# Splitting layer 1's front: batch norm and group norm two images ahead, layer norm and projection one image ahead

## The chip, the cores and the metric

The kernel runs on one core of one Trainium2 chip. The time is device microseconds (us) of one execution, the median of three runs. One more execution was profiled, with every instruction's start and end on each engine. The engines are TensorE (PE, matrix multiplies and transposes; PEld are its weight loads), VectorE (DVE), ScalarE (ACT), GpSimd (POOL) and SyncE (SP, which here issues every transfer between memory and the core's buffers).

## The reference

Four layers act on 16 images of 192 channels by 32 x 32 pixels (1024 tokens), all in float32, each as `x = x + layer(group_norm(x))`. Layer 0 is an mLSTM block with a 3 x 3 convolution and a batch norm over all images, layer 2 a depthwise convolution with batch norm, layer 3 a selective scan over four directions. Layer 1, which the change concerns, is a Mamba block on tokens:

```python
x = x + layer1(group_norm(x))            # 32 groups of 6 channels
# layer1(xf):
xn = layernorm(xf)                       # over the 192 channels
xm, z = split(xn @ in_proj_w.T)          # 384 + 384 channels
xc = silu(causal_conv1d(xm, 4 taps))
dt, B, C = split(xc @ x_proj_w.T);  dt = softplus(dt @ dt_proj_w.T + b)
h = exp(dt * A) * h + (dt * xc) * B      # a scan over 1024 tokens, 16 states
y = (sum_n h * C + xc * D) * silu(z)
out = layernorm(y @ out_proj_w.T + skip_scale * xf) @ proj_w.T + proj_b
```

## The kernel before

Each layer keeps channels on partitions (96 or 128 of them) and tokens along the free dimension. Layers 1 and 2 run together in `layer12`, one image after another. The core of it is `scan_run` (L942): one **step** is one of the 16 states of one half image (512 tokens), so an image is two units of 16 steps, 32 steps in all, and the stage has 512. A step does, for three tiles t of 128 channels, on ACT the decays (`da`, L987) and the products `xbt` (L967), on PE the transposes and a diagonal matmul into `xb` (L995, L998), on DVE the scan itself (`h`, L1011), on POOL the product with C (L1018), and two steps later on PE the sum over states into `y` (L1029). The tiles `xb` (3 PSUM buffers), `da` (5), `h` and `cb` (4) and `xbt` (2) say how far an engine can run ahead of the others.

All other work of layers 1 and 2 lies in generators that `Side.tick` (L221) advances while the steps are emitted. `side.add(kind, generator, start, end)` spreads a generator between two step numbers, in the units that its `yield`s give; `at` is 32 times the image. For an image b of the scan these are: `prep` (the projections to dt, B, C of the next unit), `gate` and `out` (the output projection of b - 1), `silu` (`layer1_gate`, the projection to z of b, L1287), `front` of b + 1, `tail` of b - 1 (layer norm, projection and residual, L1325), `conv` of b + 1 (L1263), and `layer 2` of b - 1 (L1360). That is the order of the program's text. The framework then orders each engine's queue by its own estimates of when an instruction can run; only the scan's matmuls on PE are tied to the text's order (`in_order`). On each engine the instructions then run in that order, and each waits at the head of its queue for what it needs. Side matmuls share two PSUM buffers named `mm`; the small tile `o` has two buffers, which `front` (L1257), `gate` (L1140), `tail` (L1336) and `layer 2` (L1370) take in turn.

`layer1_front` (L1223) is one generator in the kernel before. For one image it loads x into a tile called `x1` and layer 0's output into `xf` (L1227, L1229); applies layer 0's batch norm and leaky ReLU to `xf` and adds it to x (L1234 on ACT, L1235 and L1236 on DVE); stores the sum for the residual (L1238); takes group statistics (`group_norm`: L351 and L352 on DVE, L355 on PE, L357 to L362 on DVE, L365 on PE, L367 and L368 on ACT); writes the normalised image into `xf` (L1241) and stores it (L1242). From there it goes straight on to the layer norm, whose result `xn` is put into the tile `x1` again, and to the projection into the `xin` rows in memory (L1254, L1258, L1259). `xn` is read once more a good half image later, by the projection to z (L1298), and `x1` has one buffer: the next image's x can't be loaded before that projection's last matmul. The tile `xt`, also of one buffer, belongs to `out` and `tail`: it is loaded with the stored normalised image (L1311) and is free when the tail has written its own normalised image (L1352).

Of the kernel before, what the change touches and what calls it, by code (L numbers as in the profile page):

```python
# [10 lines left out]
F32 = mybir.dt.float32  # L11
# [8 lines left out]
HP = 96  # L20
DI = 384
S = 1024
# [167 lines left out]
def halves(n=S, step=512):  # L190
    return [slice(i, i + step) for i in range(0, n, step)]


def finish(steps):

    while True:
        try:
            next(steps)
        except StopIteration as end:
            return end.value  # L200
# [74 lines left out]
class Program:  # L275
# [795 lines left out]
    def layer12(self):  # L1071
        tc = self.tc
        with (
            tc.tile_pool(name="w1", bufs=1) as wp,
            tc.tile_pool(name="s1", bufs=2) as sp,
            tc.tile_pool(name="b1", bufs=2) as bp,
            tc.tile_pool(name="d1", bufs=3, space=DRAM) as dp,
            tc.tile_pool(name="ps1", bufs=2, space=PSUM) as psum,
        ):
            self.layer1_weights(wp, dp, psum)  # L1080
            self.rep = 18 * (W + 2), 6
            self.stats = wp.tile([HP, 2, 2 * self.nb, 6], F32, name="stats")
            self.image = {b: {} for b in range(self.nb)}
            side, units = Side(), []
            w_x = [self.w_x[:, t] for t in range(3)]

            def prep(u):
                xt = bp.tile([128, 4, DI], F32, name="xtok", bufs=1)
                xc = self.image[u.b]["xc"]
                rows = yield from self.scan_rows(xc[:, :, 512 * u.half : 512 * u.half + 512], w_x, 1, bp, dp, psum)  # L1090
                yield from self.scan_prep(u, rows, 0, xc, xt, True, self.w_dt, bp, psum)

            carry = [wp.tile([128, NS, 3], F32, name=f"carry{i}") for i in range(2)]
            for b in range(self.nb):
                for half in range(2):
                    c = carry[b % 2]
                    u = Unit(b, half, False, False, c if half else None, None if half else c)
                    u.neg_a = lambda t, n: self.neg_a[:, t * NS + n : t * NS + n + 1]
                    u.finish = lambda y, u=u: self.layer1_sum(u, y, bp)
                    units.append(u)  # L1100
            for b in range(self.nb):
                at = 2 * NS * b
                side.add("prep", prep(units[2 * b + 1]), at + 1, at + 13)
                if b:
                    side.add("gate", self.layer1_gated(units[2 * b - 1], bp, psum), at + 2, at + 3.5)
                    side.add("out", self.layer1_out(b - 1, bp, psum), at + 3.5, at + 8)
                side.add("silu", self.layer1_gate(b, bp, psum), at + 8, at + 12.5)
                if b + 1 < self.nb:
                    side.add("front", self.layer1_front(b + 1, sp, bp, psum), at + 12.5, at + 20)
                if b:  # L1110
                    side.add("tail", self.layer1_tail(b - 1, sp, bp, dp, psum), at + 13.5, at + 25)
                side.add("gate", self.layer1_gated(units[2 * b], bp, psum), at + 18, at + 21)
                if b + 1 < self.nb:
                    side.add("conv", self.layer1_conv(b + 1, bp, psum), at + 20, at + 26)
                if b:
                    side.add("layer 2", self.layer2(b - 1, bp, psum), at + 25.5, at + 34)
                if b + 1 < self.nb:
                    side.add("prep", prep(units[2 * b + 2]), at + 26, at + 30)
            finish(self.layer1_front(0, sp, bp, psum))
            finish(self.layer1_conv(0, bp, psum))  # L1120
            finish(prep(units[0]))
            self.scan_run(units, side, bp, psum)
            finish(self.layer1_gated(units[-1], bp, psum))
            finish(self.layer1_out(self.nb - 1, bp, psum))
            finish(self.layer1_tail(self.nb - 1, sp, bp, dp, psum))
            finish(self.layer2(self.nb - 1, bp, psum))
            self.batch_norm(sp, "2gamma", "2beta", self.bn2)
# [95 lines left out]
    def layer1_front(self, b, sp, bp, psum):  # L1223

        nc = self.nc
        x = bp.tile([HP, 2, S], F32, name="x1", bufs=1)
        nc.sync.dma_start(x, self.ins["x"][b].rearrange("(m p) t -> p m t", p=HP))  # L1227
        xf = bp.tile([HP, 2, S], F32, name="xf", bufs=1)
        nc.sync.dma_start(xf, self.y0[b].rearrange("(m p) t -> p m t", p=HP))  # L1229
        yield Wait(1)  # L1230
        for m in range(2):
            for h in halves():
                v = xf[:, m, h]
                nc.scalar.activation(v, v, AF.Identity, bias=self.bn0[:, m, 1:2], scale=self.bn0[:, m, 0:1])  # L1234
                nc.vector.scalar_tensor_tensor(v, v, 0.01, v, MUL, MAX)  # L1235
                nc.vector.tensor_tensor(x[:, m, h], x[:, m, h], v, ADD)  # L1236
                yield 0.5
        nc.sync.dma_start(self.x1[b], x)  # L1238
        mean, r, _ = yield from self.group_norm(sp, psum, x)
        for m in range(2):  # L1240
            nc.vector.tensor_scalar(xf[:, m], x[:, m], mean[:, m : m + 1], r[:, m : m + 1], SUB, MUL)  # L1241
        nc.sync.dma_start(self.xf1[b], xf)  # L1242
        yield 1
        xn = x
        for h in halves():
            yield from self.layer_norm(
                bp, psum, [xf[:, m, h] for m in range(2)], [xn[:, m, h] for m in range(2)],
                self.k("ones192", HP), HP, 512,
            )
        for t in range(3):  # L1250
            for h in halves():
                ps = psum.tile([128, 512], F32, name="mm")
                for m in range(2):
                    nc.tensor.matmul(  # L1254
                        ps, self.w_in[:, m, t * 128 : (t + 1) * 128], xn[:, m, h], start=m == 0, stop=m == 1
                    )
                o = bp.tile([128, 512], F32, name="o")  # L1257
                nc.scalar.activation(o, ps, AF.Identity, bias=self.b_in[:, t : t + 1])  # L1258
                nc.sync.dma_start(self.xin[b % 2][t][:, 3 + h.start : 3 + h.stop], o)  # L1259
                yield 1.7  # L1260
        self.image[b]["xn"] = xn
# [450 lines left out]
```

## Time and profile before

| | us |
|---|---|
| time, median of 3 runs (lowest to highest) | 17126.98 (17106.91 to 17131.63) |
| time of the profiled execution | 17158.12 |
| its span, first to last instruction | 17156.3 |
| layer 1 and 2's stage: first scan to layer 3's first scan | 3755 to 7541 |
| of this, an image in the middle (b = 8): 5534.6 to 5762.4 | 227.8 |
| layer 3: 7541 to 17156 | 9615 |

The page gives each engine's busy time and its share of the span, then the span in 40 slices, the chain that ended last, and the costliest groups of instructions. A group's line has the source line, the engine, the operation, what it writes and reads, how often it ran, then busy time, mean duration in ns, idle time of the engine before it, and what ended that. Step boundaries are the starts of the first scan (L1011 on DVE) of each step. Of the middle image b = 8: step 13 starts at 5614.3, step 17 at 5645.1, step 21 at 5690.6, step 27 at 5724.9, and the next image at 5762.4.

### The profile page before, as it was taken

The page shows a single profiled execution, that of the slowest core. Times are in us where ns is not written, and L with a number is a line of the kernel's source. Part 1 is how long each engine was busy: PE and PEld are TensorE (multiplying, and loading weights), DVE is VectorE, ACT ScalarE, POOL GpSimd, SP SyncE. Part 2 cuts the span into 40 slices and gives each one's busy share as a digit, 9 for nine tenths or more (in the row PEclk, how much of TensorE's full clock was granted, in tenths as well). Part 3 has the DMA queues.
Part 4 walks back from the last instruction along what each step waited for, and adds up shares of the span by engine and source line. Part 5 has one row for each costly group of instructions (what it writes and reads, how often), then busy time and mean ns, then how long its engine had stood idle before and what let it go on. Part 6 is the DMA issues. An engine that isn't in the chain of part 4 may idle for free. (4 is left out here: it accounts for less than half of the span.)

```text
span 17156.3 us, 262939 instructions
## 1 busy us (share of the span) xinstructions
PE 15613.4 (91%) x99452; PEld 10979.0 (64%) x99452; DVE 13102.8 (76%) x14795; ACT 11895.7 (69%) x19766; POOL 11422.4 (67%) x5491
## 2 busy tenths in 40 slices
PE   7999999979999999979999999999999999999998
PEld 4444444446555555647777777777777777777777
DVE  4555455547777777758888888988888898888888
ACT  3333333337666766748888888888888888888888
POOL 3334443436555555638888888878888888888888
PEclk8999999989999999989999999999999999999999
DMA  1111111123334443333333323333332333333232
GB/s 52 45 47 45 47 45 46 42 76 108 117 119 121 120 120 115 100 101 107 93 96 101 109 83 101 109 91 97 100 108 84 101 109 92 96 100 107 86 98 67
DMA packets 890140, 1544.64 MB, mean 90 GB/s; under 512 B 83472, under 2 KB 314653, under 8 KB 879530
## 3 DMA queue, kind: packets, MB, share of 16 engines
q1 hardware_dynamic: 888874, 1527.81, 29.7%
q8 instruction: 788, 12.91, 0.3%
q14 instruction: 478, 3.92, 0.1%
HBM read 1284.22 MB, written 243.27 MB: 89 GB/s over the span
## 5 line engine op out<-in xcount | busy, mean ns | idle before, releaser
L1018 POOL TENSOR_TENSOR h<-h,cb 128x1536 f32<-128x1536 f32 x2560 | 8871.5, 3469 | 1439.4 <-DVE h L1011 961.0
L987 ACT ACTIVATE da<-dt,neg_a 128x512 f32<-128x512 f32 x7680 | 5267.1, 714 | 1618.4 <-DVE h L1011 1565.5
L1011 DVE TENSOR_TENSOR_SCAN h<-da,carry,xb 128x512 f32<-128x512 f32 x3840 | 4653.2, 1263 | 708.8 <-PE xb L998 672.9
L1029 PE MATMUL y<-const,h 128*128 128x128 f32 x30720 | 4710.0, 276 | 127.4 <-DVE ysum L1469 54.0
L1011 DVE TENSOR_TENSOR_SCAN h<-da,xb 128x512 f32<-128x512 f32 x3840 | 4440.8, 1202 | 388.3 <-PE xb L998 272.1
L995 PE MATMUL xb<-const,xbt 128*128 128x128 f32 x23040 | 4057.7, 281 | 379.4 <-DVE h L1011 219.9
L967 ACT ACTIVATE xbt<-ut,bt 128x384 f32<-128x384 f32 x7680 | 4174.4, 603 | 210.3 <-PE xb L995 208.7
L1029 PEld LDWEIGHTS y<-const,h 128*128 128x128 f32 x30720 | 3677.9, 143 | 343.6 <-issue 288.4
L995 PEld LDWEIGHTS xb<-const,xbt 128*128 128x128 f32 x23040 | 2750.2, 142 | 1744.0 <-issue 616.2
L998 PE MATMUL xb<-diag,ut 128*128 128x128 f32 x15360 | 3015.1, 278 | 0.0
L998 PEld LDWEIGHTS xb<-diag,ut 128*128 128x128 f32 x15360 | 2382.8, 195 | 97.9 <-issue 97.9
L831 POOL TENSOR_TENSOR hs<-h,mhm 128x384 f32<-128x384 f32 x128 | 108.5, 848 | 1570.7 <-DVE den L836 735.6
L977 POOL TENSOR_TENSOR diag<-const,bt 128x512 f32<-128x512 f32 x640 | 687.0, 1074 | 575.3 <-PE xb L998 320.8
L1017 POOL COPY carry<-h 128x3 f32<-128x3 f32 x1280 | 249.1, 195 | 1222.7 <-DVE h L1011 978.2
L705 POOL TENSOR_TENSOR e<-e,const 128x1536 f32<-128x1536 f32 x128 | 443.3, 3464 | 244.0 <-DMA e<-row 226.9
L520 PE MATMUL conv<-ya,w_conv 128*64 128x512 f32 (+1 forms) x1152 | 500.9, 646 | 99.4 <-DMA ya<-yrows 61.2
L917 PE MATMUL mm<-dbl,w_dt 45*128 45x512 f32 x960 | 536.1, 642 | 33.4 <-DVE v L1491 16.1
L711 ACT ACTIVATE e<-e 128x1536 f32<-128x1536 f32 x128 | 189.7, 1482 | 445.6 <-POOL e L706 445.6
L780 PEld LDWEIGHTS num<-v,p 128*128 128x128 f32 x3072 | 386.6, 200 | 123.6 <-issue 50.8
L921 DVE SCALAR_TENSOR_TENSOR dt<-lnsq,mm 128x512 f32<-128x512 f32 x480 | 322.2, 671 | 184.1 <-ACT lnsq L920 184.1
L1172 PE MATMUL mm<-rep,taps 128*32 128x512 f32 x3072 | 423.8, 607 | 27.9 <-DMA rep<-xr 17.8
L1172 PE MATMUL mm<-rep,t_dw 96*32 96x512 f32 x2304 | 427.0, 618 | 22.1 <-DMA rep<-xr 15.9
(273 smaller groups left out, 17446.6 us busy)
## 6 DMA issues: line engine op xcount, KB each, us to landing
cb<-row SPq DMA_DIRECT2D x2560, 256.0 KB
rep<-xr SPq DMA_DIRECT2D x384, 331.0 KB
e<-row SPq DMA_DIRECT2D x128, 768.0 KB
rep<-xin SPq DMA_DIRECT2D x384, 256.0 KB
rep<-xr SPq DMA_DIRECT2D x384, 228.8 KB
x<-x SPq DMA_DIRECT2D x48, 768.0 KB
xr<-xin SPq DMA_DIRECT2D x48, 612.5 KB
xr<-xpad SPq DMA_DIRECT2D x32, 867.0 KB
```

Source lines behind the costliest of these rows:

```text
L520: nc.tensor.matmul(o, self.w_c2[:k, t, c0 : c0 + o.shape[0]], src[:k, r0 : r0 + 16, dx : dx + W], start=t == 0, stop=t == 14, skip_group_c ...
L705: nc.gpsimd.tensor_tensor(k.e, k.e, self.k0("mask")[:, None, :].to_broadcast([128, NH, 128]), ADD)
L917: nc.tensor.matmul(ps, w_dt[:, t * 128 : (t + 1) * 128], dbl, start=True, stop=True)
L967: nc.scalar.activation(t[:, c], u.ut[:, c], AF.Copy, scale=u.bt[:, c, n : n + 1])
L977: nc.gpsimd.tensor_tensor(d, ident[:, None, :].to_broadcast([128, 4, 128]), u.bt[:, 3, n : n + 4][:, :, None].to_broadcast([128, 4, 128]), ...
L987: nc.scalar.activation(da[i, t], u.dt[:, t], AF.Exp, scale=u.neg_a(t, n))
L995: in_order(nc.tensor.transpose(xb[i, t][:, c * 128 : (c + 1) * 128], xbt[i][:, c, t * 128 : (t + 1) * 128], ident))
L998: in_order(nc.tensor.matmul(xb[i, t][:, 384:], u.ut[:, 3, t * 128 : (t + 1) * 128], u.diag[n // 4][:, n % 4], start=True, stop=True, skip_ ...
L1011: nc.vector.tensor_tensor_scan(hv, dv, xv, 0.0 if first else u.carry_in[:, n, t : t + 1], MUL, ADD)
L1018: nc.gpsimd.tensor_tensor(h[i], h[i], u.c.pop(n)[:, None, :].to_broadcast([128, 3, 512]), MUL)
L1029: in_order(nc.tensor.matmul(u.y[:, j], h[i][:, t, c * 128 : (c + 1) * 128], ident, is_transpose=True, start=n == 0 and j % 4 == 0, stop=n ...
L1172: self.nc.tensor.matmul(ps[32 * g : 32 * g + 32], blocks[:, g * side + r], seen, start=r == 0, stop=r == side - 1, skip_group_check=True,)
```

## The change

`layer1_front` is cut in two. The first part ends after the group norm and the store of the normalised image; it works on the tile `xt` in place of `x1`, and leaves its `xf` to the second part. The second part, `layer1_xin`, is the layer norm and the projection; it takes `x1` for its result. No arithmetic is added or left out. The first part of image b + 2 is now emitted at steps 26.5 to 35 of image b, after the tail of b - 1 (and image 1's at steps 2 to 10 of image 0); the second part of b + 1 at 13 to 20. The yields of the first part's batch norm count 1 in place of 0.5. Other windows move: `prep` of the image's second unit from 1-13 to 0.5-12, `silu` ends at 13 in place of 12.5, `tail` from 13.5-25 to 14-26, the second `gate` from 18-21 to 18.5-22, `conv` from 20-26 to 18-24.5, `prep` of the next image from 26-30 to 24.5-29.5, `layer 2` from 25.5-34 to 26-35.

```diff
             for b in range(self.nb):
                 at = 2 * NS * b
-                side.add("prep", prep(units[2 * b + 1]), at + 1, at + 13)
+                side.add("prep", prep(units[2 * b + 1]), at + 0.5, at + 12)
                 if b:
                     side.add("gate", self.layer1_gated(units[2 * b - 1], bp, psum), at + 2, at + 3.5)
                     side.add("out", self.layer1_out(b - 1, bp, psum), at + 3.5, at + 8)
-                side.add("silu", self.layer1_gate(b, bp, psum), at + 8, at + 12.5)
+                elif self.nb > 1:
+                    side.add("front", self.layer1_front(1, sp, bp, psum), 2, 10)
+                side.add("silu", self.layer1_gate(b, bp, psum), at + 8, at + 13)
                 if b + 1 < self.nb:
-                    side.add("front", self.layer1_front(b + 1, sp, bp, psum), at + 12.5, at + 20)
+                    side.add("xin", self.layer1_xin(b + 1, bp, psum), at + 13, at + 20)
                 if b:
-                    side.add("tail", self.layer1_tail(b - 1, sp, bp, dp, psum), at + 13.5, at + 25)
-                side.add("gate", self.layer1_gated(units[2 * b], bp, psum), at + 18, at + 21)
+                    side.add("tail", self.layer1_tail(b - 1, sp, bp, dp, psum), at + 14, at + 26)
+                side.add("gate", self.layer1_gated(units[2 * b], bp, psum), at + 18.5, at + 22)
                 if b + 1 < self.nb:
-                    side.add("conv", self.layer1_conv(b + 1, bp, psum), at + 20, at + 26)
+                    side.add("conv", self.layer1_conv(b + 1, bp, psum), at + 18, at + 24.5)
+                    side.add("prep", prep(units[2 * b + 2]), at + 24.5, at + 29.5)
                 if b:
-                    side.add("layer 2", self.layer2(b - 1, bp, psum), at + 25.5, at + 34)
-                if b + 1 < self.nb:
-                    side.add("prep", prep(units[2 * b + 2]), at + 26, at + 30)
+                    side.add("layer 2", self.layer2(b - 1, bp, psum), at + 26, at + 35)
+                if b + 2 < self.nb:
+                    side.add("front", self.layer1_front(b + 2, sp, bp, psum), at + 26.5, at + 35)
             finish(self.layer1_front(0, sp, bp, psum))
+            finish(self.layer1_xin(0, bp, psum))
             finish(self.layer1_conv(0, bp, psum))
...
     def layer1_front(self, b, sp, bp, psum):
-        x = bp.tile([HP, 2, S], F32, name="x1", bufs=1)
+        x = bp.tile([HP, 2, S], F32, name="xt", bufs=1)
...
                 nc.vector.tensor_tensor(x[:, m, h], x[:, m, h], v, ADD)
-                yield 0.5
+                yield 1
...
         nc.sync.dma_start(self.xf1[b], xf)
+        self.image[b]["xf"] = xf
         yield 1
-        xn = x
+
+    def layer1_xin(self, b, bp, psum):
+
+        nc = self.nc
+        xf = self.image[b].pop("xf")
+        xn = bp.tile([HP, 2, S], F32, name="x1", bufs=1)
         for h in halves():
             yield from self.layer_norm(
```

## The prediction

> **What bounds the kernel now.** I read the page first: PE is busy for most of the span, no other engine near it.
>
> ```profile
> PE 15613.4 (91%) x99452; PEld 10979.0 (64%) x99452; DVE 13102.8 (76%) x14795; ACT 11895.7 (69%) x19766; POOL 11422.4 (67%) x5491
> ```
>
> The change touches only layer 1's stage, 3786 us of the span, so I cut its middle image (b = 8) at the step boundaries of front.md's section on the profile: steps 0-12, 13-16, 17-20, 21-26, 27-31.
>
> ```profile
> core 0: us, PE busy (x) PEld busy (x) DVE busy (x) ACT busy (x) POOL busy (x), PEclk, DMA share, GB/s
> 5534.60:5614.30 79.70, 75.53 (x468) 54.29 (x468) 58.62 (x61) 54.73 (x89) 53.47 (x31) 0.98 0.18 53
> 5614.30:5645.10 30.80, 21.75 (x126) 16.07 (x124) 29.24 (x35) 21.94 (x37) 16.97 (x10) 0.89 0.37 112
> 5645.10:5690.60 45.50, 42.34 (x193) 25.41 (x194) 29.39 (x37) 29.91 (x48) 21.30 (x9) 0.96 0.39 119
> 5690.60:5724.90 34.30, 31.48 (x204) 18.52 (x204) 30.91 (x36) 20.91 (x37) 18.79 (x7) 1.00 0.76 230
> 5724.90:5762.40 37.50, 36.70 (x237) 21.74 (x235) 24.04 (x27) 30.61 (x47) 19.31 (x8) 1.00 0.54 149
> ```
>
> Four stretches are PE's (93 to 98% busy). Steps 13-16 are not: PE 21.75 of 30.8, DVE 29.24. Four steps take 30.8 us there, 9 of them without PE. The table of PE's waits over eleven images (b = 3 to 13, 4399.6 to 6894.9) says who ends that idleness:
>
> ```profile
> engine line waited for: us in total, times, longest us
> PE mm L355 <- DVE gnmv L352: 56.8, 11, 5.2
> PE mm L1065 <- ACT o L1258: 24.9, 11, 2.4
> PE mm L1298 <- ACT xtok L933: 23.1, 33, 0.9
> PE y L1029 <- ACT ysum L1131: 22.8, 11, 2.1
> PE mm L1273 <- DMA rep<-xin: 17.1, 19, 2.2
> PE xb L995 <- DVE gnd L359: 16.3, 11, 1.5
> PE mm L377 <- DVE xf L1241: 15.8, 22, 1.5
> ```
>
> Three of these rows are the front's chain: 56.8 + 16.3 + 15.8 = 88.9, or 8.1 us an image. The timeline of image 8 (SP, then DVE) shows why:
>
> ```profile
> 5612.31 0.42 SPq L1227 DMA_DIRECT2D x<-x  x1
> ...
> 5618.66 5.54 DVE L1236 TENSOR_TENSOR x<-x,xf 96x512 f32<-96x512 f32 x4 [0.94 <-DMA x<-x]
> 5624.13 1.87 DVE L351 BATCH_NORM_STATS2 gnst<-x 96x6 f32<-96x512 f32 x3
> ...
> 5627.94 0.16 DVE L357 COPY gnmean<-mm 96x2 f32<-96x2 f32 x1
> ...
> 5633.84 3.53 DVE L1241 TENSOR_SCALAR xf<-x,gnmean,gnr 96x1024 f32<-96x1024 f32 x2
> ```
>
> x is asked for only when z's projection has freed `x1`, lands 6.35 us later, and from 5618.66 to 5628.0 DVE runs no scan. PE stands at L355, with the next scan matmuls behind it.
>
> **What the skill says.** The Trainium skill, "TensorE: Matmul & The Clock Gate", on engine queue depths: only weight loads overtake on PE, and DVE and ACT are strict FIFO. The trace agrees: 5.2 us at L355, no later matmul meanwhile. "SBUF — State Buffer", on its two separate sides: a DVE operation with two SBUF inputs and a GpSimd operation lock each other out for a whole instruction. The trace agrees: the first L1236 took 3.73 us, the next three 0.68 each, while L1018 ran 3.47 us from 5618.38. "DMA: Bandwidth & Descriptors", rules for kernel authors: issue early, wait late. That is the mechanism claimed here.
>
> **The change, part by part**, per image. That it does nothing can be excluded: in the built order, DVE's adds into `xt` stand after the third scan of step 27 and around the first two of step 28, the statistics in 28-29, L357 to L362 in steps 0 and 1 of the next image, the normalisation (there L1245) in step 1, and steps 13-16 hold layer norms and z's SiLU only.
>
> *Removed from 13-16:* DVE 5.54 (L1236) + 2.50 (L351) + 0.39 (L352) + 0.16 + 0.39 (five small ones) + 3.53 (L1241) = 12.5 us, leaving 16.7; PE's 21.75 and ACT's 21.94 remain. No engine has over 22 us, so 30.8 goes to about 22: -9. Bounds: -9.5 (all of PE's idle 9.05 and a little of the 0.89 clock), and -6 if z's SiLU (two table loads of 1.28 and 2.77 on ACT, 5.3 us), which hid beside x's load, comes to light.
>
> *Added to 27-31 and the next 0-1:* 8.4 of the 12.5 us fall in 27-29: DVE 24.04 + 8.4 = 32.4 of 37.5, below PE. Single steps get DVE-bound (step 28: scans 3.7, four side operations of 0.68 and more). +1, bounds 0 and +3.
>
> *x's load* now waits for the tail's L1352, step 25. Seven scans and some side operations stand between it and the first add. At 1.2 us a scan that is 8.4 us at the very least, and it needs 6.35 us, plus up to 3.4 if it shares with the xr store (768 KB at the 230 GB/s that the stretch 21-26 moved, an estimate). Steps 25-27 took 3.5, 4.2, 9.7 before, so it is covered: 0, bound +2. *Layer 2's replica loads* queue behind it on SP: from xr's store (5715.45) to the first L1172 (5726.48) were 11.0 us; as many steps lie between now: 0, bound +3.
>
> *The residual load in the tail (L1337).* Before, it was issued in steps 4-5, 90 us ahead, since `o` was free. In the new order its `o` is the one that the first `xin` store reads: SP stands until that store has landed (3.4 us: store 5659.50, reader issued 5662.88), then the load takes 2.8 (5686.42 to 5689.26, where DVE idled 3.03 for the second half's). DVE's L1345, after the first scan of step 18, waits, two scans queue behind it, and behind these PE's `xb`. ACT's four batch norm pieces (0.8 each) that DVE also waits for cover part: 6.2 less about 4. +2, bounds 0 and +6.
>
> *SiLU of xc* moves from 27, where PE had layer 2 to do, to 24, with less: +0.5 (bounds 0, +3). *prep* an image earlier by 1.5 steps takes 6 + 6 of PE's wide matmul rows (L888 and L917, some 5 us) out of the fullest stretch: -1 (0, -2). *conv* two steps nearer to its projection: its waits (17.1 / 11 = 1.6) stay: 0, bound +2. *The xf store and the load into `xt`* for `out` come in steps 1-3 and are used in step 5, more than 10 us later against 6.4: 0.
>
> Sum: -9 + 1 + 2 + 0.5 - 1 = -6.5 us. The stall occurs in images 0 to 14: 15 x -6.5 = -97.5; image 0 gets two fronts, +3. The profiled execution was 17158.1 (span 17156.3, 1.8 around it), so 17063.6, or 0.9945 of it; the runs' median 17127.0 gives **17032 us**.
>
> **Rivals.**
> *(a) The wait only moves.* DVE, at 172 of 227.8 us an image, pays the 12.5 us in steps 28-29 and 1, PE stands at the layer 2 loads, and 9 becomes 8 lost: -1 an image, -15 + 3 = -12, 17115, within the noise. For it: DVE locked by L1018 (3.47 us of each step) can be held at each add, which are now apart. Against: the adds stand between scans, and PE has 27-29's layer 2.
> *(b) Slower: the `o` chain.* If POOL is late in step 17, SP holds the store back behind a `cb` load (L969 waits for L1018, 3.5 us), and both residual halves make DVE wait: 3.4 + 2.8 + 3.5, then again 3.4 + 2.8 for the second, less what ACT covers. From 9 us of waiting an image on it eats the gain; at 13 the sum is +4.5: 15 x 4.5 + 3 = +70.5, 17197. For it: two-buffer `o`, SP in order. Against: PE is full in steps 17-20 (42.34 of 45.5), so DVE's wait costs only beyond `xb`'s three buffers.
> *(c) Larger gain.* With ACT and DVE relieved at 13-16, the waits at L1065 (2.3 an image) and L1298 shrink also: -11, 15 x -11 + 3 = -162, 16965.
>
> **Chances and range.** Forecast (-3.5 to -9.5 an image, 16988 to 17078) 0.54, (c) 0.16, (a) 0.14, (b) 0.16. 0.2% is about what a measurement of this kernel tells from no change (34 us): faster 0.70, same 0.14, slower 0.16. The range from 16960 to 17170 takes in (a), nearly all of (c) and the near half of (b). All upper bounds at once (-6 + 3 + 2 + 3 + 6 + 3 + 2 = +13 an image) it doesn't hold: they would have to fall together; the forecast's own is 16988 to 17078.
>
> **What would show it.** Right: L355's wait of 5.2 gone from PE's table; an image at about 221 us; steps 13-16 near 22 us; DVE's adds at steps 27-28 with idle below 1 us before them. Wrong: L1345's line (then L1355) with several us idle on the residual load in step 18; layer 2's matmuls waiting for `rep`; ACT's SiLU at step 24 with PE idle beside it; a step 1 of over 10 us at L1245. If the image stays at 227 with 13-16 short, (a) holds.

## The result: 0.24% faster, where 0.55% was forecast

The changed kernel took 17085.65 us (median of 14 runs, 17056.51 to 17092.28) against 17123.86 for the kernel before (14 runs, 17106.68 to 17138.46): a ratio of 0.9976, 95% interval 0.9968 to 0.9983; the medians are 38 us apart. Timed once more beside later runs (e10 below) it gave 0.9966, 0.9953 to 0.9978, with medians 57 us apart. The forecast was 17032, -95 us, so the first measurement is 0.4 of it and the second 0.6. The sign held, and the wait at L355 went as forecast; the size did not hold. The changed kernel's profiled execution took 17092.28 us, its span is 17090.5.

The page's first part: PE is busy 65 us less than before, DVE 31 us more.

```profile
PE 15548.9 (91%) x99452; PEld 10964.4 (64%) x99452; DVE 13134.0 (77%) x14795; ACT 11874.2 (69%) x19766; POOL 11420.7 (67%) x5491
```

Layer 1's stage (first scan of layer 1 to first scan of layer 3) went from 3785.4 to 3722.4 us; the rest of the program took 10 us less ahead of it and 7 us more behind it, which says little: between any two of the profiles of this document these parts differ by up to 15 and 23 us. Its images go against the forecast in an odd way: images 3 to 8 take 226.8 us on the mean, as before (227.1), and images 9 to 13 take 220.6, which is what was forecast (221). So I cut both an image of the first kind (b = 8) and one of the second (b = 11) at the same five stretches as before: steps 0-12, 13-16, 17-20, 21-26, 27-31. Image 8 of the changed kernel (stretch, its length, then busy time and count of PE, PE's weight loads, DVE, ACT, POOL, the granted clock, DMA share, GB/s, as in the table of before):

```profile
5501.75:5586.98 85.23, 77.34 (x483) 53.92 (x482) 66.95 (x67) 55.04 (x93) 54.40 (x32) 0.98 0.22 67
5586.98:5611.32 24.34, 21.29 (x129) 14.88 (x128) 18.88 (x21) 22.53 (x36) 17.08 (x10) 1.00 0.25 76
5611.32:5653.63 42.31, 38.61 (x193) 23.67 (x192) 28.41 (x33) 28.49 (x47) 18.46 (x8) 0.96 0.45 143
5653.63:5693.88 40.25, 36.14 (x213) 21.61 (x212) 31.53 (x36) 24.93 (x38) 20.32 (x8) 0.92 0.63 197
5693.88:5727.94 34.06, 30.49 (x208) 19.88 (x207) 30.80 (x34) 25.35 (x45) 19.11 (x7) 0.95 0.49 142
```

And the first stretch of image 11, whose other four are within 1.5 us of these:

```profile
6168.86:6247.71 78.85, 75.47 (x483) 53.60 (x482) 62.22 (x68) 55.16 (x93) 54.45 (x32) 1.00 0.24 73
```

Before, the five were 79.7, 30.8, 45.5, 34.3, 37.5. Steps 13-16 have lost 6.5 us, not 9. Steps 21-26 have grown by 6, 27-31 lost 3.4, 17-20 lost 3.2. And the two kinds of image differ mainly in steps 0-12, by 6.4 us (7.2 on the mean): the place to which the front's group norm has moved. The table of PE's waits over the same eleven images (b = 3 to 13) has lost L355, L1065 and the front's L377, and has new rows on top (us in total, times, longest):

```profile
PE mm L365 <- DVE gnq L362: 63.4, 17, 4.5
PE mm L932 <- DVE dt L921: 33.4, 10, 3.3
...
PE mm L1264 <- DVE xt L1355: 23.9, 11, 2.8
...
PE xb L995 <- ACT xbt L967: 16.6, 24, 1.3
```

17 waits at L365 in eleven images: eleven are the tail's (2.7 to 3.4 us each, in step 25 by its scans, which the expectations below call step 24), six are the front's (4.5 us each). The timelines of DVE and then PE in image 8, step 0 and the start of 1, show one of the six:

```profile
5506.61 3.22 DVE L359 TENSOR_TENSOR gnd<-gnmv,gnmean 96x2 f32<-96x2 f32 x1
5509.76 1.20 DVE L1011 TENSOR_TENSOR_SCAN h<-da,xb 128x512 f32<-128x512 f32 x1
5510.89 0.13 DVE L361 TENSOR_TENSOR gnq<-gnd 96x2 f32<-96x2 f32 x1
5510.94 1.21 DVE L1011 TENSOR_TENSOR_SCAN h<-da,xb 128x512 f32<-128x512 f32 x1
5512.07 0.13 DVE L362 TENSOR_TENSOR gnq<-gnq,gnmv 96x2 f32<-96x2 f32 x1
```

```profile
5512.34 0.30 PE L365 MATMUL mm<-gnq,const 96*96 96x2 f32 x2 [4.51 <-DVE gnq L362]
5512.57 4.47 PE L888 MATMUL mm<-xc,w_x 128*45 128x512 f32 x6
```

In image 11 the same instructions stand in another order, the three small ones together:

```profile
6171.62 1.30 DVE L359 TENSOR_TENSOR gnd<-gnmv,gnmean 96x2 f32<-96x2 f32 x1
6172.95 0.16 DVE L361 TENSOR_TENSOR gnq<-gnd 96x2 f32<-96x2 f32 x1
6173.15 0.16 DVE L362 TENSOR_TENSOR gnq<-gnq,gnmv 96x2 f32<-96x2 f32 x1
```

In image 8 two scans lie between L359 and L362, and L365, which waits for L362, stands ahead of L888 and the next `y` matmuls on PE: 4.5 us of nothing, then what was held up follows. In image 11 L362 is done at 6173.31 and L365 starts at 6174.25 with no wait. The normalisation behind it (L1245) differs too; here it is on DVE in image 8 and in image 11, then POOL in image 8:

```profile
5513.74 3.90 DVE L1245 TENSOR_SCALAR xf<-xt,gnmean,gnr 96x1024 f32<-96x1024 f32 x1 [0.42 <-ACT gnr L368]
6178.20 1.53 DVE L1245 TENSOR_SCALAR xf<-xt,gnmean,gnr 96x1024 f32<-96x1024 f32 x2 [0.94 <-ACT gnr L368]
```

```profile
5506.38 3.43 POOL L1018 TENSOR_TENSOR h<-h,cb 128x1536 f32<-128x1536 f32 x1
5513.66 3.44 POOL L1018 TENSOR_TENSOR h<-h,cb 128x1536 f32<-128x1536 f32 x1
```

In image 8 the first half of the normalisation alone lasts 3.90 us beside L1018; in image 11, where an L1018 has just ended (at 6178.22), both halves take 1.53. In images 3 to 8 steps 0 to 2 take 23.3 to 24.6 us, in images 9 to 14 they take 16.9; L359 and the first L1245 are 1.9 and 3.1 us longer in the first kind, in every image of it.

In the built order one can count beforehand how L365 stands to L362: the number of scan turns (L998) ahead of L365 on PE, less the number of scans ahead of L362 on DVE. I call it the lead. It is 1 in images 3 to 8 and 3 in images 9 to 14. My theory after the look at L365 alone: with a lead of 1 the group norm costs PE 6 us an image, with 2 or more next to nothing; and that is the larger part of what is missing. The rival: images 3 to 8 are slow for another reason, such as the DMA queues that their loads fall on.

### The profile page after: what moved, and what is told of

Its sections match the earlier page's. It is cut to its first block, busy times and chain, and to the rows that moved or that the text cites. A ratio compares the mean times of both kernels' runs of the same rounds, so it can differ in the third digit from the quotient of the medians.

```text
span 17090.5 us, 263059 instructions
## 1 busy us (share of the span) xinstructions
PE 15548.9 (91%) x99452; PEld 10964.4 (64%) x99452; DVE 13134.0 (77%) x14795; ACT 11874.2 (69%) x19766; POOL 11420.7 (67%) x5491
## 5 line engine op out<-in xcount | busy, mean ns | idle before, releaser
L1018 POOL TENSOR_TENSOR h<-h,cb 128x1536 f32<-128x1536 f32 x2560 | 8874.8, 3470 | 1582.5 <-DVE h L1011 1004.8
L995 PE MATMUL xb<-const,xbt 128*128 128x128 f32 x23040 | 4060.1, 281 | 372.0 <-DVE h L1011 220.3
L995 PEld LDWEIGHTS xb<-const,xbt 128*128 128x128 f32 x23040 | 2752.6, 142 | 1825.7 <-issue 645.4
L998 PE MATMUL xb<-diag,ut 128*128 128x128 f32 x15360 | 3008.3, 278 | 0.0
L998 PEld LDWEIGHTS xb<-diag,ut 128*128 128x128 f32 x15360 | 2376.5, 195 | 54.8 <-issue 54.8
L569 PE MATMUL mm<-xn,w_up 96*128 96x512 f32 x768 | 404.6, 673 | 34.6 <-DVE xn L389 22.2
```

Of the source, the lines that this page charges most:

```text
L995: in_order(nc.tensor.transpose(xb[i, t][:, c * 128 : (c + 1) * 128], xbt[i][:, c, t * 128 : (t + 1) * 128], ident))
L998: in_order(nc.tensor.matmul(xb[i, t][:, 384:], u.ut[:, 3, t * 128 : (t + 1) * 128], u.diag[n // 4][:, n % 4], start=True, stop=True, skip_ ...
L1018: nc.gpsimd.tensor_tensor(h[i], h[i], u.c.pop(n)[:, None, :].to_broadcast([128, 3, 512]), MUL)
```

## Experiments

Each run is timed against the kernel before on its own chip; e1 to e4 shared a chip, e5 to e8 another, e9 to e11 a third. The table gives the ratio to the kernel before with its interval, and from each run's own profile the stage of layer 1 and the mean of images 3 to 13 by stretch.

| run | ratio (95%) | stage us | 0-12 | 13-16 | 17-20 | 21-26 | 27-31 | image |
|---|---|---|---|---|---|---|---|---|
| before | 1 | 3785.4 | 78.9 | 30.8 | 44.8 | 34.3 | 38.0 | 226.8 |
| changed | 0.9976 (0.9968-0.9983) | 3722.4 | 82.7 | 24.6 | 41.9 | 40.3 | 34.4 | 224.0 |
| e1 front from 27 | 0.9969 (0.9957-0.9981) | 3721.4 | 85.2 | 24.6 | 41.4 | 40.5 | 31.7 | 223.4 |
| e2 front to 34.5 | 0.9954 (0.9941-0.9966) | 3695.0 | 80.2 | 24.4 | 42.1 | 40.3 | 34.5 | 221.4 |
| e3 three `o` | 0.9955 (0.9942-0.9967) | 3702.2 | 82.6 | 24.3 | 38.9 | 40.7 | 34.7 | 221.4 |
| e4 split alone | 0.9954 (0.9941-0.9966) | 3709.2 | 81.4 | 23.9 | 43.0 | 34.4 | 39.5 | 222.2 |
| e5 three in one | 0.9913 (0.9899-0.9926) | 3632.1 | 79.0 | 24.3 | 39.0 | 38.7 | 34.4 | 215.4 |
| e6 changed, no SiLU of z | 0.9929 (0.9917-0.9942) | 3651.9 | 83.1 | 21.8 | 39.4 | 40.1 | 34.4 | 218.8 |
| e7 before, three `o` | 0.9976 (0.9966-0.9986) | 3715.7 | 78.5 | 30.8 | 40.0 | 34.5 | 38.8 | 222.6 |
| e8 before, moves alone | 1.0017 (1.0009-1.0026) | 3795.6 | 78.6 | 30.6 | 44.5 | 40.0 | 33.9 | 227.7 |
| e9 before, no SiLU of z | 1.0003 (0.9995-1.0011) | 3777.0 | 78.4 | 30.7 | 45.4 | 33.8 | 38.1 | 226.5 |
| e10 changed again | 0.9966 (0.9953-0.9978) | 3724.1 | 82.9 | 24.5 | 41.9 | 40.7 | 34.4 | 224.4 |
| e11 changed, no front add | 0.9926 (0.9912-0.9940) | 3647.6 | 82.5 | 24.3 | 42.3 | 40.1 | 29.3 | 218.6 |

### e1 and e2: the order of the group norm

```diff
-    side.add("front", self.layer1_front(b + 2, sp, bp, psum), at + 26.5, at + 35)
+    side.add("front", self.layer1_front(b + 2, sp, bp, psum), at + 27, at + 35)      # e1: lead 1 in images 3-14
+    side.add("front", self.layer1_front(b + 2, sp, bp, psum), at + 26.5, at + 34.5)  # e2: lead 2 in images 3-14
```

> The first part of the front gets the window 27 to 35 in place of 26.5 to 35; nothing else differs. In the built order PE's matmul L365 of the front stands one scan behind DVE's L362 in all of the images 3 to 14 (in the changed kernel: one scan in 3 to 8, three in 9 to 14). Order theory (PE stands at L365 wherever only one scan lies between, and nowhere else): images 9 to 14 go from 220.5 to 226.5 us, 6 x 6 = +36 us, so 17085.7 + 36 = 17122, ratio to the kernel before 0.9999. Rival (images 3 to 8 are slow for another reason, such as the DMA queues that their loads fall on): images 9 to 14 stay at 220.5, 17086, ratio 0.9978.

> The first part of the front gets the window 26.5 to 34.5 in place of 26.5 to 35. In the built order L365 of the front then stands two scans behind L362 in the images 3 to 14. Order theory: images 3 to 8 go from 226.5 to 220.5 us, 6 x -6 = -36 us, so 17050, ratio to the kernel before 0.9957; L365's wait on L362 in steps 0 and 1 is below 1 us an image. Rival (another reason): images 3 to 8 stay at 226.5, 17086, ratio 0.9978.

e1, image 11, steps 0-12: 78.85 in the changed kernel, here

```profile
6155.07:6240.23 85.16, 77.27 (x483) 54.08 (x482) 66.96 (x68) 55.05 (x93) 54.36 (x32) 0.98 0.23 68
```

e2, image 8, steps 0-12: 85.23 in the changed kernel, here

```profile
5477.00:5557.06 80.06, 75.75 (x483) 53.49 (x482) 63.93 (x68) 54.96 (x93) 54.41 (x32) 1.00 0.25 72
```

Both ways round the order theory holds where it looks: with a lead of 1 steps 0-12 of images 9 to 13 go from 78.8 to 85.9, with a lead of 2 those of images 3 to 8 go from 86.0 to 80.0. PE's waits in images 9 to 13 count ten at L365 in e1 (39.3 us), two an image, and five in the changed kernel (16.8 us). The slow images moved with the order, so the rival's DMA queues are out. The whole of e1 did not lose the 36 us, though: its images are 223.4, because 27-31 fell to 31.7. Half a step later two of the front's adds stand ahead of the last `dt` in place of three, and PE's waits for that `dt` (L932) fell from 33.4 to 15.6 us in the eleven images. That was a second cost of the change that I had not in view, and e11 measures it.

What is shown is that the order costs these microseconds, not that the wait at L365 alone does. Half a step moves the whole front, and L359 and L1245 change their lengths with it. In images 3 to 7 of e1 the lead is 1 and L365 waits only 1.1 us, yet steps 0 to 2 take 20.9 us, 4.0 more than with a lead of 3. In image 3 of e5 (below) L365 waits for nothing, L1245 lasts 3.83 us, and steps 0 to 2 take 21.5 us against 18.0 in that run's next image. Nor does a lead of 1 cost the same everywhere: in images 4 to 13 the tail's L365 has it in all of these kernels, and waits 3.4 us in the changed kernel, 0.8 to 0.9 us in the kernel before, and not at all in e4 and e7, where no scan stands between its L359 and L362.

In e2 the stage is 27.4 us below the changed kernel's, not 36; with a lead of 2, steps 0-12 of images 9 to 13 are 1.7 us longer than with 3, so 2 is not quite enough: from image 5 on L365 still waits 0.9 to 1.2 us there.

### e3 and e7: the residual load and the two buffers of `o`

The same edit on the changed kernel (e3) and on the kernel before (e7); `o` is allocated in four places. To make room, layer 1's small group norm tiles have one buffer in place of two in both runs (and in e5), which was not tried apart.

```diff
-    o = bp.tile([128, 512], F32, name="o")
+    o = bp.tile([128, 512], F32, name="o", bufs=3)
```

> The changed kernel with three buffers of the tile o in place of two (the group norm's small tiles of layer 1 take one buffer each in place of two, to make room). The orders of the front are those of the changed kernel. The residual load L1347 then need not wait for a store that reads o. Theory of the residual load: PE's waits on L1355 (2.3 us at L1264 in step 18, 1.2 us at L1283 in step 21 in every image) go, 15 x -2 to -3.6 = -30 to -54 us, so 17032 to 17056. Rival (the four batch norm pieces on ACT and DVE that stand in the same steps set the time, and the load is only the last to be named): the wait goes to another name, 17086.

> The kernel before with three buffers of the tile o (and one each of the group norm's small tiles in layer 1). Theory (the residual load's wait was made by the change): nothing of the 2.4 to 3.3 us of steps 17 to 20 that the same edit took in the changed kernel, 0 to -1 us an image from the wait at L1065, ratio 0.9990 to 1.0000. Rival (two buffers of o cost the kernel before as much): -2.5 us an image, ratio 0.9978.

e3, image 8, steps 17-20, 42.31 in the changed kernel:

```profile
5613.01:5651.82 38.81, 36.99 (x193) 22.37 (x192) 28.42 (x34) 28.18 (x47) 18.33 (x8) 1.00 0.49 157
```

e7, image 8, steps 17-20, 45.50 in the kernel before; PE 39.55 of 39.67:

```profile
5605.19:5644.86 39.67, 39.55 (x185) 23.66 (x186) 30.06 (x37) 29.80 (x48) 21.28 (x9) 1.00 0.42 136
```

e3 gives 3.0 us an image in 17-20, as its theory said. DVE's L1355 in image 11 of the changed kernel is the wait that the forecast described:

```profile
6288.88 0.75 DVE L1355 SCALAR_TENSOR_TENSOR xt<-mm,b_proj,o 96x512 f32<-96x512 f32 x1 [2.60 <-DMA o<-x1d]
```

But e7's rival is right: two buffers cost the kernel before more still, 4.8 us in 17-20. There PE waited 2.3 us an image at L1065 for the `o` of L1258, and DVE 2.8 us at L1345 for the second half's residual load, as much as the 2.7 us at L1355 in the same stretch of the changed kernel. In e7 the first is gone and of the second 0.3 us an image is left. So the residual load is no new cost. The change turned one form of the same shortage into another and came out about 2 us ahead. One buffer more in the kernel before is worth about as much as the whole change (0.9976, beside 0.9976 and 0.9966).

### e4 and e8: the two halves of the change

e4 is e2 with every other window put back to that of the kernel before; e8 is the kernel before with the moved windows and the front in one piece. The lines that carry them:

```diff
-    side.add("conv", self.layer1_conv(b + 1, bp, psum), at + 18, at + 24.5)
-    side.add("prep", prep(units[2 * b + 2]), at + 24.5, at + 29.5)
+    side.add("conv", self.layer1_conv(b + 1, bp, psum), at + 20, at + 26)
+    side.add("prep", prep(units[2 * b + 2]), at + 26, at + 30)
```

> The front is split as in the changed kernel, its first part in the window 26.5 to 34.5 (as in the run with 34.5, with which it is compared), but every other window is that of the kernel before. Forecast's theory (the moved windows are worth +0.5 - 1 = -0.5 us an image): steps 21 to 26 go back to about 34 us and 27 to 31 to about 38, and the sum is 8 us above to 8 below the run with 34.5. Rival A (the moves cost: the trace shows 7 us more of PE's waits in steps 24 to 27): -2.3 us an image, 35 us below the run with 34.5, about 17015. Rival B (the moves make room for the front in DVE's queue): steps 27 to 31 go over 42 us, +4 us an image, 60 us above, about 17110.

> The kernel before with the moved windows of the changed kernel and the front in one piece (13 to 20). In the built order L365 of the front stands one scan behind L362 in step 15 (two in the kernel before). Forecast's theory (the moved windows are worth -0.5 us an image): ratio 0.9990 to 1.0005. Rival (they cost 5.6 us in steps 21 to 26 and only give it back where the front has left steps 13 to 16): +3 us an image, ratio 1.0026. The wait of 5 us at L355 stays in both.

The split is the gain. With the old windows (e4) the image is 222.2, with the new ones (e2) 221.4, medians 17079.7 and 17074.8: the forecast's reading of the moves as about nothing stands beside the split. Alone (e8) they cost 0.17%, outside the forecast's range and nearer to its rival: 21-26 take 5.7 us more and 27-31 give back 4.1. In e8 PE's waits at L365 for L362 come to 39.2 us in images 3 to 13, up to 3.4 each, against 10.4 in the kernel before; in e4 the tail's L365 hardly waits: the tail's wait belongs to the moves, not to the split. e4 also shows the split's terms by themselves, against the kernel before: -6.9 in 13-16, -1.8 in 17-20, +0.1 in 21-26, +1.5 in 27-31, +2.5 in 0-12. There L932 waits 0.3 us an image for `dt`, against 3.0 in the changed kernel: that wait comes only of the split and the earlier `prep` together.

### e6 and e9: the SiLU of z

Left out in both: the SiLU of z and its two table loads, so the gate multiplies by z itself. e6 is the changed kernel without it, e9 the kernel before.

```diff
-        self.silu(sz)
```

> The changed kernel without the SiLU of z: the activation in layer1_gate and its two table loads are left out, so the gate multiplies by z itself; the orders of the front are unchanged. ACT is then free of 5.3 us (1.28 + 2.77 + 1.28) in steps 12 and 13. Theory (the SiLU that had hidden beside x's load comes to light in the changed kernel, which is why 13 to 16 went to 24.4 and not to 22): steps 13 to 16 go from 24.4 to about 22, -2 to -3 us an image, 16 x -2.4 = -38 us, so about 17048, ratio to the kernel before 0.9955. Rival (the layer norms' chain over DVE, ACT and PE sets the 24.4): 13 to 16 stay above 24.

> The kernel before without the SiLU of z (its activation and two table loads left out, the gate multiplies by z). Theory (in the kernel before the SiLU hides beside x's load in steps 12 and 13): steps 13 to 16 stay at 30.8, within 1 us, and the edit takes less than half of what it took in the changed kernel, 0 to -2.4 us an image, ratio 0.9978 to 1.0000. Rival (the SiLU costs both kernels the same): -4.5 us an image as in the changed kernel, ratio 0.9959.

e6, image 8, steps 13-16:

```profile
5558.52:5580.32 21.80, 20.90 (x129) 14.89 (x128) 18.70 (x21) 17.79 (x32) 16.55 (x10) 1.00 0.30 79
```

e9, image 8, steps 13-16, where ACT is just as much relieved:

```profile
5600.85:5631.65 30.80, 21.64 (x128) 16.91 (x127) 27.63 (x36) 17.88 (x33) 17.79 (x10) 0.83 0.40 114
```

In the kernel before the SiLU was free: 30.8 with and without, ratio 1.0003. In the changed kernel it costs 2.8 us in 13-16 and 2.5 more in 17-20, twice what the expectation had (ratio 0.9929, not 0.9955). ACT's timeline of the changed kernel, image 11, shows the hole that PE falls into:

```profile
6246.88 1.28 ACT L1294 ACT_TABLE_LOAD   x1
6248.18 2.77 ACT L1294 ACTIVATE sz<-sz 128x3072 f32<-128x3072 f32 x1
6250.95 1.28 ACT L1295 ACT_TABLE_LOAD   x1
6252.24 1.12 ACT L967 ACTIVATE xbt<-ut,bt 128x384 f32<-128x384 f32 x2
```

For 5.36 us ACT makes no `xbt`; PE's L995 waits 1.5 of them (16.6 us in eleven images, the row above); by what way the rest of the 5.2 us is lost was not followed. The 21.8 without it is what the forecast took for the stretch.

### e11: the adds in DVE's queue

Left out: the front's addition of x, so that x1 is x alone.

```diff
-                nc.vector.tensor_tensor(x[:, m, h], x[:, m, h], v, ADD)
```

> The changed kernel without the front's four additions to x in DVE's queue (L1240 left out, so x1 is x alone); the orders of the front are unchanged. Theory (one of the adds stands 3.4 us beside POOL's L1018, with dt's L921 behind it, and PE's L932 waits 3.3 us for that dt): steps 27 to 31 go from 34.5 to about 31, -3 us an image, -45 us, ratio 0.9950. Rival (the load of x or the stores in SP's queue are late, or PE has another wait behind this one): 34, ratio 0.9975.

e11, image 8, steps 27-31, 34.06 in the changed kernel:

```profile
5665.31:5694.34 29.03, 28.90 (x208) 18.93 (x207) 25.38 (x31) 25.25 (x45) 18.66 (x7) 1.00 0.70 184
```

In the changed kernel the four adds cost 5.1 us an image in this stretch (the expectation had 3), where the forecast had +1 for all of the front's work on DVE in 27-31 and the next 0-1. DVE's timeline of the changed kernel, image 11, step 27 and start of 28:

```profile
6361.80 3.36 DVE L1240 TENSOR_TENSOR xt<-xt,xf 96x512 f32<-96x512 f32 x1
6365.09 1.26 DVE L1011 TENSOR_TENSOR_SCAN h<-da,carry,xb 128x512 f32<-128x512 f32 x1
...
6368.05 0.66 DVE L921 SCALAR_TENSOR_TENSOR dt<-lnsq,mm 128x512 f32<-128x512 f32 x1
```

and POOL's:

```profile
6360.69 3.93 POOL L1018 TENSOR_TENSOR h<-h,cb 128x1536 f32<-128x1536 f32 x1
```

The first add had taken 1.11 us; the second lasts 3.36 us beside L1018, and behind it in DVE's queue stand two scans, the third add and the last `dt` (L921), for which PE's L932 waits (33.4 us in ten times). The Trainium skill, "SBUF — State Buffer", two separate sides, says of such a pair that the one that starts second blocks until the other is done; the add's end at 6365.16, 0.54 us after L1018's at 6364.62, agrees (the third add, alone, took 0.66). That PE waited for the adds' place is shown by e1 and e11; that the lock made most of it is read from these lines and was not tried apart. In image 8 of e4 an add lasts 3.21 us beside L1018 too, but no `dt` stands close behind it, and 27-31 is only 1.5 us longer than in the kernel before.

### e10: how much of the difference is chance

> The changed kernel as it is, beside the others on this chip: which part of the difference between the profiles (-63 us in layer 1's stage) and the medians (-38 us) is chance. If the profile of the kernel before was a long one: the stage again 3722 within 10 us, ratio 0.9965 to 0.9980. If that of the changed kernel was a short one: a stage of about 3745.

The stage came out at 3724.1, so the changed kernel's profile was a typical one. The profile of the kernel before, at 17158.1, lies above all its 14 timed runs, and e9, whose median is that of the kernel before within 0.03%, has a stage of 3777.0: some 8 of the 63 us between the first two profiles may be chance, or more, since the medians give 38 and 57. The intervals of the two ratios, 0.9976 and 0.9966, overlap.

### e5: a version that is faster than both

Three buffers of `o`, the front in the window 27 to 36 (lead 2 or 3), and one step of waiting ahead of the tail's L365:

```diff
-    side.add("front", self.layer1_front(b + 2, sp, bp, psum), at + 26.5, at + 35)
+    side.add("front", self.layer1_front(b + 2, sp, bp, psum), at + 27, at + 36)
 ...
         nc.vector.tensor_tensor(q, q, mv[:, :, 1], ADD)
         yield 1
+        if lead:
+            yield Wait(lead)
```

> Three edits to the changed kernel together: three buffers of o (as in the run e3), the front's first part in the window 27 to 36 (two scans between L362 and L365 in images 3 to 14, and its adds behind the dt of prep), and one step of waiting before the second matmul L365 of the tail's group norm (two scans there, one in the changed kernel). Theory (each wait that the trace names is time): step 0 to 1 -5 us in six images, step 17 to 20 -2.8, step 27 -3, step 24 -3 an image: an image of about 214 us against 226.7 before, 15 x -12.7 = -190 us on the kernel before, ratio 0.9890. Rival (the waits in steps 24 and 27 have another one behind them, as L365 had L888): -8 an image, -120 us, ratio 0.9930.

The median is 16979.4, the ratio 0.9913, about three times the change's own gain. The image is 215.4, and L365 is gone from the top of PE's waits, whose first rows are now these (line numbers are 2 higher in this kernel):

```profile
PE mm L387 <- ACT lnsq L386: 25.0, 33, 1.1
PE xb L997 <- DVE h L1013: 20.8, 11, 2.7
```

The rival had a part: of the tail's 3.4 us at L365 only 1.6 came back in 21-26, where `xb` now waits 1.9 us an image for `h`, and 27-31 kept its 34.4 although e1 with its start at 27 had 31.7.

## Why the prediction was wrong in size

Step by step, as the sum put it.

- **"13-16 goes to about 22: -9".** It went to 24.6: -6.2. The lower bound given there, -6 "if z's SiLU comes to light", is what happened, and for that reason (e6 against e9). Before, the SiLU ran beside x's load; with the load gone its 5.4 us on ACT count. Adding busy times (no engine over 22 us, so 22) took ACT's 21.94 to be spread over the stretch, but 5.36 of it stand in one block, and `xbt` has two buffers.
- **"Added to 27-31 and the next 0-1: +1", "SiLU of xc +0.5, prep -1".** This is the step that failed most. The three stretches that these terms speak of, 21-26, 27-31 and 0-12, together grew by 6.2 us an image (+6.0, -3.6, +3.8), where the terms have +0.5. The forecast compared sums of busy time (DVE 32.4 of 37.5, so below PE), priced each operation at its own duration and each term apart. It left out how long PE stands when one of its in-order matmuls has its producer late in DVE's queue. Three such waits appeared: at L365 of the front in images 3 to 8, whose order costs 6 us in each of these (e1, e2; e2 got 27 us of the stage back); at L365 of the tail, 3.3 us an image, made by the moved windows (e4, e8); and at L932, 3.0 us an image, where the adds stand ahead of `dt` (the adds cost 5.1 in all, e11), which comes only of the split and the moved `prep` together. For the split alone the term was low but not far off: +1.5 and +2.5 in e4 against bounds of 0 and +3.
- **One image for fifteen.** The sum took one image's figure 15 times; the built order is not the same in every image. Why the framework turns the order over at image 9 was not found. Image 0, which the forecast made 3 us longer for its two fronts, went from 190.7 to 180.9 us; why was not looked into.
- **"The residual load: +2".** The wait is there (2.2 us at L1264 an image, e3 gives back 3.0), but the same two buffers had cost 4.8 before (e7), the wait for a residual load among it. Steps 17-20 went down by 2.9 and not up: the mechanism was right, and its counterpart in the kernel before was missed, though the forecast showed the row (L1065, 24.9) and named DVE's 3.03 us.
- **conv 0.** PE's waits for `rep<-xin` did not stay, as forecast, but fell from 17.1 to 2.0 us in eleven images; 11.5 us at the same matmul, L1283, for the tail's L1355 came in their place.
- **x's load, layer 2's loads, the `xf` store and load: 0.** No row of PE's waits names them in the changed kernel, and none of DVE's names x's load; right.
- **Signs.** L355's wait is gone, as said under "right". Of the signs under "wrong", a step 1 of over 10 us came in image 8 (10.5 us, 6.1 in image 11), and L1355's idle on the residual load.
- **Sum.** With the order put right (e2) an image is 221.4, -5.4 against the -6.5 of the forecast, but not by its terms: 13-16 has -6.4, 17-20 -2.7, 27-31 -3.5, 21-26 +6.0 and 0-12 +1.3. That the sum comes near is in part luck. The changed kernel as it stands has 224.0, -2.8. Of the rivals, (a) described images 3 to 8 well: image unchanged, DVE held by L1018. It named the wrong victim, layer 2's matmuls, where it was L365 and L932.

Three slips in the forecast's readings change nothing in it: PE is 92% busy in steps 21-26, not 93 or more; the group norm's small operations L357 to L362 are four, not five; and the 768 KB are x's own size, the xr store has 867.

## What to carry to other kernels

When an operation chain of several engines is moved, look in the built order, in every repetition, at each matmul that waits for it: how many turns PE is ahead of the producing engine there, what stands between the links of the chain, and which large operation of another engine will run beside them. The lead is a warning and not a price: with a lead of 3 this group norm cost nothing, with a lead of 1 some 6 us, and elsewhere a lead of 1 cost between 0 and 3.4. Price the moves together, since two that are cheap apart (the split in e4, an earlier `prep`) made a new wait at L932. When a stall is removed, ask what ran free beside it (here a SiLU with two table loads, 0 us before, 5.2 after), and when a buffer wait is forecast for the new kernel, look for the same shortage in the old one.

## What was unexpected in the hardware

A subtraction of 96x2 numbers, L359, took 3.22 us beside POOL's L1018 in image 8 and ended with it (5509.83 and 5509.81); in image 11 it took 1.30, again up to the end of an L1018, where L361 and L362 took 0.16 each. What such an operation costs was set by what ran beside it, not by its size. From the start of L359 in image 8 to the end of L362 are 5.6 us: 3.2 of L359 and two scans of 1.2. PE stood for the last 4.5 of them; how much each of the two bears was not tried apart. ACT's two table loads took 1.28 us each, with gaps of 0.02 us before and after.
